# Twelve edge tiles of the first sums, moved from among the last blocks to behind them

## The chip, the cores and the metric

The kernel runs on one core of a Trainium2 chip. The core has a matrix engine (PE, with its weight loads shown apart as PEld), a vector engine (DVE), a scalar engine (ACT), GpSimd (POOL) and a queue processor (SP); transfers run on 16 DMA engines that all queues share. Each engine works through its own list of instructions in order and waits where an input is not there yet. The metric is the device time of one execution in microseconds; lower is better.

## The reference

Two message-passing layers over a graph of 3125 nodes (256 features) and 50000 edges (16 features), sorted by `dst`. The change lies in the first:

```
h   = relu(layernorm(x))
m   = relu(concat(h[src], h[dst], e) @ mW1 + mb1)      # per edge, 512 wide; src is called i, dst j
agg = segment_sum(m @ mW2 + mb2, src)                  # per node
u   = relu(concat(h, agg) @ uW1 + ub1) @ uW2 + ub2
x   = x + h + u
```

It is followed by three graph convolutions over the same edges, with degree scaling, bias and gelu, added to x again. The kernel uses that `segment_sum(m @ mW2)` is `segment_sum(m) @ mW2`, so that only the relu of each edge has to be summed per source node.

## The kernel before

**Two tables, and edges sorted by source.** `h @ mW1` is split by its inputs: `tabA` holds h times the rows for the source, `tabB` h times the rows for the target plus bias. An edge's hidden row before the relu is `tabA[src] + tabB[dst] + e @ wE`. The 50000 edges come as 66 *blocks* of 768 (six groups of 128; the last block holds 80 edges). For each block the kernel forms `tabB[dst] + e @ wE` on PE with one-hot matrices (L642 to L657), copies the result out of PSUM (L660) and scatters it by POOL (L661), six scatters of 128 rows of 528 floats, into `rows_d`, sorted by *node tile*: 25 tiles of 125 source nodes, each with room for 17 groups of 128 edges. A row carries its edge's source and target number behind the 512 values. `window(b)` loads the part of `tabB` that the block needs three blocks ahead on SP's queue (L617); `features(b)` loads edge features on ACT's queue.

**The first sums.** When 26 blocks have been placed, the first 640 rows (`KP` = 5 groups) of every node tile are in place, since later blocks only fill later groups. So from block 26 on a generator, `first_sums`, works on these five groups of each node tile while the other blocks go on. Per node tile t it loads the rows (`xz`, L724, 1320 KB) and 125 rows of `tabA` (L731, 250 KB) on SP's queue, one tile ahead, into two buffers that take turns: the load for tile t+1 has to wait until tile t-1 has been read for the last time. Then come the tile's own steps: target numbers `d_of` (L766), the table rows split in two halves (L245, L246), one-hot matrices of the sources (L769, L770), their transposes on PE (L777, L779), and a copy kept for later in `oh_d` (L781, L782). Then five *edge tiles*, one per group, each one step of the generator: PE spreads the `tabA` rows to the edges (L251), DVE adds the scattered rows (L253, `gb`), ACT and DVE form the relu in two halves `m` (L255, L256), and PE adds them into `p_sum` (L756), one edge tile behind. After the fifth the sum is copied and stored to `R_d` (L759, L760). That makes 25 x 5 = 125 edge tiles.

**Who sets the order.** The generator is advanced by the loop over the blocks: from block `SUMS_AT` = 29 on, after each block, as many steps are taken as the pacing line asks for:

```
if b >= SUMS_AT:
    while n_sums > NT * KP - NT * KP * (b + 1 - SUMS_AT) // (NB - SUMS_AT):
```

Over 37 blocks that is 125 edge tiles, three or four a block, and the last four follow block 65. Program order is not yet the order on the engines: the framework orders each engine's list when the kernel is built, by program order but with steps drawn forward where by its own estimate their inputs are ready. In the trace a tile's `d_of` stands on DVE ahead of the previous tile's third edge tile.

**After the blocks.** A count of failed conditions (L824 to L827) gives `flag`; the branch on it (L1398) starts `messages`, the *message stage*, which has the other twelve groups of each node tile to do (edge tiles again, with L253 to L256 and L1017), counts edges for the second layer and updates the nodes. It loads rows of `rows_d` (L918), which need all scatters in place. Nothing in it can be drawn ahead of the branch. Last come the convolutions, `gcn`.

Of the kernel before, what the change touches and what calls it, by code (L numbers as in the profile page):

```python
# [46 lines left out]
NT, NP = 25, 125  # L47
# [6 lines left out]
NB = (E + BLK - 1) // BLK  # L54
# [6 lines left out]
KP = 5  # L61
FULL_AT = 26
SUMS_AT = 29
MID = 1024
NG, AW = 7, 448
NPAD = NG * AW
# [35 lines left out]
def gnn(ctx: ExitStack, tc: tile.TileContext, x, src, dst, ea, mW1, mb1, mW2, mb2, uW1, ub1, uW2,  # L102
# [160 lines left out]
    with s1:  # L263
# [185 lines left out]
        for a in range(0, NT, TG):  # L449
# [4 lines left out]
            nc.tensor.matmul(p[:, :n], ones_h[:NB, :], Xv[:, v], start=False, stop=True)  # L454
            nc.vector.tensor_scalar(base[:, v], p[:, :n], float(-MID), None, op0=ALU.add)

# [19 lines left out]
        same = l1.tile([P, CN], F32, name="same")  # L476
        nc.gpsimd.tensor_scalar(same, real, float(MID), None, op0=ALU.mult)
        nc.gpsimd.tensor_add(same, same, peers)
# [114 lines left out]
        def features(b0):  # L593
            st[b0] = g1.tile([P, EB, MB * ED], F32, name="ea_st", bufs=2)
            n = min(EB, NB - 1 - b0)
            nc.scalar.dma_start(
                st[b0][:, :n, :].rearrange("p b (h v) -> p (b h) v", h=2),
                ea[b0 * BLK:(b0 + n) * BLK, :].rearrange("(b p j) f -> p b (j f)", p=P, j=MH))
            if b0 + EB >= NB:
                last = st[b0][:, NB - 1 - b0, :]  # L600
                nc.vector.memset(last, 0.0)
                nc.scalar.dma_start(last[P - LEFT:, (MB - 1) * ED:], ea[FULL:, :])
# [4 lines left out]
        def window(b):  # L607
            if b % WG == 0:
                w_now[0] = g1.tile([1, WG, 2], I32, name="w_now", bufs=2)
                c = nc.vector.tensor_copy(w_now[0], w0_i[0:1, b:b + WG, :])  # L610
                if b:
                    tc.add_manual_dep(c.ins, w_now[1].ins.name, SYNC, reason="one group ahead")
            rows, tab = (64 if b < WIDE else P), tabB[b >= EARLY]
            for h in range(2) if b < NB - 1 else (1,):
                reg = nc.sync.value_load(w_now[0][0:1, b % WG, h:h + 1], min_val=0,
                                         max_val=tab.shape[0] - rows)
                o = nc.sync.dma_start(bw[(2 * b + h) % RW][P - rows:, :].bitcast(F32),  # L617
                                          tab[bass.ds(reg, rows), :])
            if b % WG == 0:
                w_now[1] = o  # L620

        def prepare(b):

            rows = pcs[b % 2]
            pc = rows[:, :MB * 64].rearrange("p (k a b f) -> p k a b f", k=MB, a=2, b=2)
            v = st[b // EB * EB][:, b % EB, :].rearrange("p (j f) -> p j f", f=ED)
            v = v.unsqueeze(2).to_broadcast([P, MB, 2, ED])
            nc.vector.tensor_copy(pc[:, :, :, 0, :], v)
            nc.vector.tensor_sub(pc[:, :, :, 1, :], v, pc[:, :, :, 0, :].bitcast(F32))
            rows = rows.bitcast(F32)  # L630
            one[b] = g1.tile([P, MB, P], F32R, name="ohd", bufs=2)
            pay[b] = one[b] if b < WIDE else pays[b % 2]
            a, of = (64, of_high) if b < WIDE else (0, of_row)
            for h in range(2):
                c = slice(h * MH, (h + 1) * MH)
                t = gps.tile([P, H], F32, name="tr")
                for j in range(MH):
                    q = (h * MH + j) * 64
                    nc.tensor.transpose(t[:, j * P:(j + 1) * P], rows[:, q:q + P], ident)
                nc.scalar.copy(pay[b][:64, c, :].rearrange("q j e -> q (j e)"), t[:64, :MH * P])  # L640
                t = gps.tile([P, H], F32, name="bc")
                nc.tensor.matmul(t[:, :MH * P], ident_h[:NB, b:b + 1].to_broadcast([NB, P]),  # L642
                                 near[:, c, :].rearrange("b j p -> b (j p)"), start=True, stop=True)
                made[b] = nc.vector.tensor_scalar(one[b][a:, c, :].rearrange("q j p -> q (j p)"),
                                                  t[a:, :MH * P], of[a:, 0:1], None, op0=ALU.is_equal)

        def block(b):
            z = zt[b % RZ]
            cols = range(MB) if b < NB - 1 else (MB - 1,)
            c = nc.gpsimd.tensor_copy(z[:, :, H:H + 2], ends[:, :, b, :])  # L650
            if b:
                tc.add_manual_dep(c.ins, evicted[b - 1].ins.name, SYNC, reason="scatters before it first")
            for j in cols:
                p = gps.tile([P, H], F32, name="p_z", bufs=3)
                if b >= WIDE:
                    nc.tensor.matmul(p, pay[b][:, j, :], wE, start=True, stop=False)
                nc.tensor.matmul(p, one[b][:, j, :], bw[(2 * b + j // MH) % RW], start=b < WIDE,  # L657
                                 stop=True)
                by = nc.vector.tensor_copy if b < FULL_AT and j in (2, 3) else nc.scalar.copy
                evicted[b] = by(z[:, j, :H], p)  # L660
                s = nc.gpsimd.indirect_dma_start(  # L661
                    out=rows_d, in_=z[:, j, :], in_offset=None,
                    out_offset=bass.IndirectOffsetOnAxis(ap=place[:, j, b:b + 1], axis=0))
                placed(s, b >= FULL_AT)
# [14 lines left out]
        def free_places(t):  # L679
            if t == 0:  # L680
                nc.gpsimd.iota(free_i, pattern=[[1, ND]], base=0, channel_multiplier=ND)
                nc.vector.tensor_copy(free[0], free_i)
                nc.vector.tensor_scalar(free[1], free[0], n_of[:, 0:1], None, op0=ALU.add)
                nc.vector.tensor_scalar(before[:, 0:1], n_of[:, 0:1], -1.0, float(CAP), op0=ALU.mult,
                                        op1=ALU.add)
                return
            nc.vector.tensor_scalar(free[2], free[0], before[:, t - 1:t], n_of[:, t:t + 1],
                                    op0=ALU.is_ge, op1=ALU.mult)
            nc.vector.tensor_add(free[1], free[1], free[2])
            if t < NT - 1:  # L690
                nc.vector.scalar_tensor_tensor(before[:, t:t + 1], before[:, t - 1:t], float(CAP),
                                               n_of[:, t:t + 1], op0=ALU.add, op1=ALU.subtract)
            else:
                nc.vector.tensor_copy(free_i, free[1])

        def no_edges(c):
            with tc.issue_after(scatters[-1].ins):
                s = nc.gpsimd.indirect_dma_start(
                    out=rows_d, in_=zero, in_offset=None,
                    out_offset=bass.IndirectOffsetOnAxis(ap=free_i[:, c:c + 1], axis=0))  # L700
            placed(s, True)
# [95 lines left out]
        for b in range(NB):  # L797
            if b % EB == 0 and b + EB < NB:
                features(b + EB)
            if b + AHEAD < NB:  # L800
                window(b + AHEAD)
            if b + 1 < NB:
                prepare(b + 1)
            if b == FULL_AT:
                ready += scatters
                assert len(ready) == FULL_AT * MB
                sums, n_sums = first_sums(), NT * KP
                next(sums)
            block(b)
            for t in range(5 * b - 5, 5 * b) if 0 < b <= NT // 5 else ():  # L810
                free_places(t)
            if NB - 2 - ND <= b < NB - 2:
                no_edges(b - (NB - 2 - ND))
            for v, n in work:
                while len(v) > max(0, n - n * (b + 1) // FULL_AT):
                    v.pop(0)()
            if b >= SUMS_AT:
                while n_sums > NT * KP - NT * KP * (b + 1 - SUMS_AT) // (NB - SUMS_AT):
                    next(sums)
                    n_sums -= 1  # L820
        assert next(sums, None) is None

        t = small()
# [608 lines left out]
```

## Time and profile before

| what | value |
|---|---|
| median of 4 runs | 2063.13 us (2058.87 to 2065.77) |
| profiled execution | 2065.86 us, its span 2064.1 us |
| first edge tile of the first sums, `gb` | 361.58 us |
| last scatter of the last block | 775.04 us |
| last step of the last edge tile ends | 779.47 us |
| first load of the message stage | 784.89 us |
| first load on the chain of the second layer | 1533.09 us |
| PE, DVE, ACT, POOL busy over the span | 87%, 62%, 52%, 23% |
| blocks 17 to 27, without sums | 7.78 us each |
| blocks 29 to 65, with 125 edge tiles | 414 us together |

How to read the lines of the profile: `L253` is a line of the kernel; `gb<-xz,p_x` is output from inputs; `x2` merges neighbours of the same kind; a bracket gives the idle time before an instruction and what ended it. In a table by stretches each engine's busy time is followed by the number of its instructions, then come the granted clock of PE, the share of the 16 DMA engines that was busy, and GB/s. `SPq` and `ACTq` are transfers being issued by these queues.

### The profile page before, as it was taken

The page shows a single profiled execution, that of the slowest core. Times are in us where ns is not written, and L with a number is a line of the kernel's source. Part 1 is how long each engine was busy: PE and PEld are TensorE (multiplying, and loading weights), DVE is VectorE, ACT ScalarE, POOL GpSimd, SP SyncE. Part 2 cuts the span into 40 slices and gives each one's busy share as a digit, 9 for nine tenths or more (in the row PEclk, how much of TensorE's full clock was granted, in tenths as well). Part 3 has the DMA queues.
Part 4 walks back from the last instruction along what each step waited for, and adds up shares of the span by engine and source line. Part 5 has one row for each costly group of instructions (what it writes and reads, how often), then busy time and mean ns, then how long its engine had stood idle before and what let it go on. Part 6 is the DMA issues. An engine that isn't in the chain of part 4 may idle for free. (4 is left out here: it accounts for less than half of the span.)

```text
span 2064.1 us, 28354 instructions
## 1 busy us (share of the span) xinstructions
PE 1795.2 (87%) x9183; PEld 1410.1 (68%) x9183; DVE 1278.8 (62%) x2931; ACT 1068.0 (52%) x2214; POOL 482.2 (23%) x562
## 2 busy tenths in 40 slices
PE   4788585776767786999999999999979999999997
PEld 1433243454545554788888888888867998999996
DVE  6987243665556566989998889898823233323332
ACT  3445254665656673556555556565536344434432
POOL 6467777655545550000000000000000000000000
PEclk8789797878889897999999999999989999999998
DMA  5679898888888876445454444544221000000111
GB/s 159 232 292 338 316 324 307 300 292 298 296 303 305 314 266 222 159 145 159 149 163 147 144 162 145 162 154 154 87 76 47 1 1 1 1 1 8 34 38 49
DMA packets 182238, 348.27 MB, mean 169 GB/s; under 512 B 38384, under 2 KB 67936, under 8 KB 181690
## 3 DMA queue, kind: packets, MB, share of 16 engines
q1 hardware_dynamic: 112790, 191.30, 29.4%
q0 software_dynamic: 34560, 117.58, 14.9%
q10 hardware_dynamic: 34724, 37.42, 5.3%
q8 instruction: 76, 1.25, 0.2%
q14 instruction: 88, 0.72, 0.1%
HBM read 187.51 MB, written 158.66 MB: 168 GB/s over the span
## 5 line engine op out<-in xcount | busy, mean ns | idle before, releaser
L1278 PE MATMUL p_o<-a,g 125*128 125x448 f32 x2100 | 460.0, 374 | 3.6 <-ACT g L1263 3.4
L661 POOL DMA_INDIRECT rows_d<-zt,place x391 | 393.3, 1006 | 251.7 <-issue 135.5
L1278 PEld LDWEIGHTS p_o<-a,g 125*128 125x128 f32 x2100 | 392.2, 188 | 42.2 <-ACT g L1263 4.6
L255 ACT ACTIVATE m<-gb 128x512 fp32r<-128x512 f32 x425 | 265.5, 632 | 153.8 <-DVE gb L253 111.1
L256 DVE SCALAR_TENSOR_TENSOR m<-gb,m 128x512 fp32r<-128x512 f32 x425 | 287.4, 688 | 31.0 <-ACT m L255 28.5
L1273 ACT CAST a<-A 125x448 fp32r<-125x448 uint8 x263 | 148.6, 566 | 229.3 <-PE p_o L1278 227.8
L1273 DVE CAST a<-A 125x448 fp32r<-125x448 uint8 x262 | 102.8, 393 | 233.3 <-PE p_o L1278 232.3
L1017 PE MATMUL p_sum<-m,oh 128*125 128x512 f32 x600 | 235.8, 436 | 3.1 <-ACT m L255 1.6
L974 PE MATMUL p_A<-od,oh_h 128*126 128x448 f16 (+3 forms) x1000 | 237.4, 327 | 1.2 <-ACT of_src L1005 1.2
L251 PE MATMUL p_x<-apc,ohT 125*128 125x512 f32 x600 | 236.1, 466 | 1.3 <-ACT ohT L950 0.7
L253 DVE TENSOR_TENSOR gb<-z,p_x 128x512 f32<-128x512 f32 x300 | 202.2, 683 | 34.9 <-PE p_x L251 33.6
L660 ACT COPY zt<-p_z 128x512 f32<-128x512 f32 x339 | 182.9, 587 | 63.0 <-PE p_z L657 57.9
L657 PE MATMUL p_z<-bw,ohd 128*128 128x512 f32 x391 | 169.2, 482 | 35.9 <-ACT t_sb L345 16.5
L1226 POOL DMA_DIRECT2D wG<-in_L_gnn_W x3 | 2.2, 745 | 757.4 <-ACT rs_t L218 755.0
L756 PE MATMUL p_sum<-m,hT 128*125 128x512 f32 x250 | 113.6, 501 | 53.9 <-DVE m L256 51.8
L657 PEld LDWEIGHTS p_z<-bw,ohd 128*128 128x128 f32 x391 | 80.2, 215 | 103.5 <-issue 34.8
L974 PEld LDWEIGHTS <-oh_h 128*126 128x126 f16 x1000 | 125.5, 137 | 35.0 <-issue 1.0
L1017 PEld LDWEIGHTS p_sum<-m,oh 128*125 128x125 f32 x600 | 112.3, 189 | 43.9 <-ACT m L255 17.8
L960 DVE TENSOR_SCALAR od<-iota_h,dloc 128x447 f16<-128x447 f16 (+11 forms) x300 | 138.7, 488 | 0.0
L998 ACT CAST A<-p_A 126x448 uint8<-126x448 f32 x175 | 92.9, 531 | 59.5 <-PE p_A L974 58.0
L251 PEld LDWEIGHTS p_x<-apc,ohT 125*128 125x128 f32 x600 | 109.4, 193 | 12.9 <-ACT ohT L950 1.7
L338 PE MATMUL p_z<-wAB,hT 128*128 128x512 f32 (+1 forms) x200 | 108.4, 678 | 8.5 <-ACT hT L321 4.3
(280 smaller groups left out, 2792.0 us busy)
## 6 DMA issues: line engine op xcount, KB each, us to landing
z<-rows_d SPq DMA_DIRECT2D x75, 1056.0 KB
xz<-rows_d SPq DMA_DIRECT2D x25, 1320.0 KB
tabB<-t_sb ACTq DMA_DIRECT2D x26, 512.0 KB
bw<-tabB SPq DMA_DIRECT2D x51, 256.0 KB
bw<-tabB SPq DMA_DIRECT2D x80, 128.0 KB
rows_d<-zt,place POOLq DMA_INDIRECT x391, 6.2
hT<-tabA SPq DMA_DIRECT2D x25, 250.0 KB
R_d<-R_part ACTq DMA_DIRECT2D x25, 250.0 KB
```

What stands on the lines that cost most here:

```text
L251: nc.tensor.matmul(p, ohT, apc[:NP, s, :], start=s == 0, stop=s == 1)
L253: nc.vector.tensor_add(gb, zr, p)
L255: nc.scalar.activation(m[:, 0, :], gb, AF.Relu)
L256: nc.vector.scalar_tensor_tensor(m[:, 1, :], gb, 0.0, m[:, 0, :].bitcast(F32), op0=ALU.max, op1=ALU.subtract)
L657: nc.tensor.matmul(p, one[b][:, j, :], bw[(2 * b + j // MH) % RW], start=b < WIDE, stop=True)
L660: evicted[b] = by(z[:, j, :H], p)
L661: s = nc.gpsimd.indirect_dma_start(out=rows_d, in_=z[:, j, :], in_offset=None, out_offset=bass.IndirectOffsetOnAxis(ap=place[:, j, b:b + 1 ...
L960: nc.vector.tensor_scalar(targets[k][:, :WIDTH[k]], iota_h[:, :WIDTH[k]], d_of[:, t, k:k + 1] if k < KP else dloc[t][:, k:k + 1], None, op ...
L974: nc.tensor.matmul(p_A[g][:, l - g * AW:h - g * AW], oh_h[t][:, k, :], targets[k][:, l - FIRST[k]:h - FIRST[k]], start=start, stop=stop)
L1017: nc.tensor.matmul(p_sum[t], oh, m[:, s, :], start=k == KP and s == 0, stop=k == KT - 1 and s == 1)
L1273: (nc.vector.tensor_copy if turn[0] % 2 else nc.scalar.copy)(a, A[:NP, s, j * AW:(j + 1) * AW])
L1278: nc.tensor.matmul(po[:, f, :AW], g[:, s, q, f * P:(f + 1) * P], a, start=s == 0 and q == 0, stop=s == NT - 1 and q == 1)
```

## The change

A constant `REST_OF` = 12 is added. The pacing line spreads 125 - 12 = 113 edge tiles over blocks 29 to 65, and the twelve that are left are taken one after another behind the last block: the last two of node tile 22 and all ten of tiles 23 and 24. Every instruction of the kernel is still there once.

```
+REST_OF = 12
...
             if b >= SUMS_AT:
-                while n_sums > NT * KP - NT * KP * (b + 1 - SUMS_AT) // (NB - SUMS_AT):
+                while n_sums > NT * KP - (NT * KP - REST_OF) * (b + 1 - SUMS_AT) // (NB - SUMS_AT):
                     next(sums)
                     n_sums -= 1
+        for _ in range(n_sums):
+            next(sums)
         assert next(sums, None) is None
```

## The prediction

> **What bounds the kernel now.** I read the page's forty slices first, to see that the change sits in one stage: slices 7 to 15 (about 360 to 780 us), where the last 37 blocks of edges run beside the first sums. No engine is full there and the DMA engines come nearest, so I asked next for the busy time in stretches of 50 us, then of 3 us.
>
> ```profile
> 600.00:650.00 50.00, 32.59 (x141) 23.16 (x139) 26.38 (x53) 27.07 (x54) 24.81 (x29) 0.87 0.86 306
> 650.00:700.00 50.00, 39.10 (x162) 28.26 (x162) 31.62 (x60) 32.88 (x67) 27.05 (x30) 0.85 0.85 302
> ...
> 711.00:714.00 3.00, 1.78 (x8) 1.07 (x7) 0.00 (x0) 3.00 (x8) 2.09 (x4) 1.00 1.04 416
> 714.00:717.00 3.00, 0.00 (x0) 0.00 (x0) 0.90 (x4) 0.37 (x1) 2.42 (x4) 0.79 1.05 417
> 717.00:720.00 3.00, 2.24 (x6) 1.39 (x6) 3.00 (x7) 0.50 (x1) 2.31 (x2) 0.50 0.62 247
> 720.00:723.00 3.00, 3.00 (x10) 2.32 (x9) 1.28 (x3) 1.82 (x5) 0.73 (x1) 0.57 0.50 192
> ```
>
> The columns are PE, weight load, DVE, ACT, POOL, granted clock, DMA share and GB/s. Over 50 us the DMA engines are 86% busy at some 305 GB/s. Inside that they swing: full while DVE does nothing (711 to 717 us), half idle just after. The waits from 380 to 860 us say what DVE stands for.
>
> ```profile
> DVE d_of L766 <- DMA xz<-rows_d: 99.5, 21, 11.3
> PEld p_sum L756 <- DVE m L256: 80.0, 50, 11.5
> POOL rows_d L661 <- ACT zt L660: 62.3, 53, 11.0
> ```
>
> DVE waits 4.7 us per node tile for the tile's rows (L724), and PE and POOL wait behind it. Last, the time line around the end of the stage, DVE, SP, POOL and ACT alone:
>
> ```profile
> 752.03 0.38 SPq L724 DMA_DIRECT2D xz<-rows_d  x1
> 758.10 1.28 DVE L253 TENSOR_TENSOR gb<-xz,p_x 128x512 f32<-128x512 f32 x2 [0.69 <-PE p_x L251]
> 763.06 0.17 DVE L766 TENSOR_TENSOR d_of<-xz,first 128x5 f32<-128x5 f32 x1 [2.88 <-DMA xz<-rows_d]
> 775.04 0.98 POOL L661 DMA_INDIRECT rows_d<-zt,place  x1 [1.54 <-issue]
> 778.18 1.29 DVE L256 SCALAR_TENSOR_TENSOR m<-gb,m 128x512 fp32r<-128x512 f32 x2
> 780.68 0.27 ACTq L760 DMA_DIRECT2D R_d<-R_part  x1
> 784.89 0.30 SPq L926 DMA_DIRECT2D a_rows<-tabA  x1
> ```
>
> The rows of node tile 24 are asked for at 752.03, when tile 22 has let go of its buffer. Tile 24's first step (763.06) stands on DVE behind only two of tile 23's five edge tiles, so three of them wait for that load too. The last scatter goes out at 775.04, the last edge tile ends at 779.47, its sums are stored at 780.68, and the message stage starts at 784.89, when that store has landed. So the end of the edge tiles sets the start of the next stage, and nothing is left to wait for on POOL.
>
> **The change, part by part.** The pacing line has 113 edge tiles to spread over blocks 29 to 65 and not 125, 3.05 a block and not 3.38. Twelve tiles, 2.4 node tiles of five, come after block 65: the last two of tile 22, and all of 23 and 24. The instructions are the same in number, the flag's steps and the store before the branch keep their place at the end, and the gap from 779.47 to 784.89 stays: 0. So the sum has two terms: what the blocks' stretch loses, and what the tail costs.
>
> *What 2.4 node tiles are worth among the blocks.* From one d_of to the next, from 400.98 to 763.06 us, are 21 periods of 17.24 us with 186 scatters, 8.86 (1.48 blocks) in each. Four neighbours show how they vary; from the first to the fourth they hold 6, 15 and 3 scatters.
>
> ```profile
> 648.21 0.17 DVE L766 TENSOR_TENSOR d_of<-xz,first 128x5 f32<-128x5 f32 x1 [5.98 <-DMA xz<-rows_d]
> 661.20 0.20 DVE L766 TENSOR_TENSOR d_of<-xz,first 128x5 f32<-128x5 f32 x1 [2.17 <-DMA xz<-rows_d]
> 684.39 0.17 DVE L766 TENSOR_TENSOR d_of<-xz,first 128x5 f32<-128x5 f32 x1 [7.55 <-DMA xz<-rows_d]
> 696.77 0.22 DVE L766 TENSOR_TENSOR d_of<-xz,first 128x5 f32<-128x5 f32 x1
> ```
>
> The trace doesn't show a node tile's price by itself, so three ways bound it. (1) By bytes: a node tile moves 1320 KB of rows, 250 of table, 250 of sums and 157.5 of one-hots, 2.025 MB; a block moves six scatters of 270 KB, two windows of 256 KB and 48 KB of features, 2.195 MB. Together 2.025 + 1.48 x 2.195 = 5.27 MB in 17.24 us, 305 GB/s, which is what the stretches show. So a node tile is 6.6 us. (2) By POOL: blocks 17 to 27, without sums, took 7.78 us each, six scatters of 0.96 us with 0.30 between and a copy; 17.24 - 1.48 x 7.78 leaves 5.7 us. (3) A straight line through the periods against their scatters gives 8.5 us + 0.99 us per scatter. I take the bytes, 6.6, because they reproduce the period and DMA is the resource nearest to full. The blocks' stretch ends 2.4 x 6.6 = 15.9 us earlier; ends 13.7 and 20.4. SP's queue is asked for tile 24's rows later, with only the branch behind; ACT's for the stores of tiles 22 to 24, where nothing waits for them but the last.
>
> The Trainium skill, page "DMA: Bandwidth & Descriptors", speaks against the change here: by "Issuing engines are not separate DMA queues" all queues share the same 16 engines, and its Specifications give them a ceiling of 435 GB/s. At that ceiling the 4.86 MB of 2.4 node tiles are worth 11.2 us, and the change would cost 4.7 us more than my sum. The 3 us rows do reach 416 and 417 GB/s, but only in the stretches in which DVE stands; the mean of 305 is what a longer stretch gets.
>
> *What twelve tiles cost alone.* With nothing else on DVE an edge tile takes 1.335 us: the message stage runs pairs of them so.
>
> ```profile
> 800.95 1.28 DVE L253 TENSOR_TENSOR gb<-z,p_x 128x512 f32<-128x512 f32 x2
> 802.41 1.29 DVE L256 SCALAR_TENSOR_TENSOR m<-gb,m 128x512 fp32r<-128x512 f32 x2 [0.19 <-ACT m L255]
> 803.62 1.28 DVE L253 TENSOR_TENSOR gb<-z,p_x 128x512 f32<-128x512 f32 x2
> ```
>
> Two pairs stand 2.67 us apart. Tile 22's last two are 2.7 us. Tile 23: its end is held by tile 24's load, which starts when tile 22 has ended, takes 7.3 us at the least (583.60 to 590.87), then 1.1 us of first steps (0.17, 0.16 and 0.80, partly over each other), then three edge tiles, 4.0: 12.4 us. The shortest period of the trace, 684.39 to 696.77, is 12.4 as well. Tile 24 has no load behind it: five edge tiles, 6.7, and 1.65 of its own steps, 8.3 us. Sum 23.4 us. The low end has the load hidden and 8.3 us for both, 19.3; the high end 12.4 for both, 27.5. None of it has cover: the last scatter lands some 6.2 us (the median of their landings) after its issue, long before the branch, and the stage behind the branch cannot start early. In before the same four tiles stand behind block 65's scatter as in the new order stand ahead of the twelve, so that part cancels.
>
> The same page's "Anatomy of one DMA" fits a transfer of POOL's path with 2.0 us + bytes / 436 GB/s, 5.1 us for these 1320 KB; tile 23 would then take 10.2 us and the sum would be 2.2 us smaller. No load of rows whose landing shows in this stage was that quick, and all had scatters beside them.
>
> **The sum.** 23.4 - 15.9 = +7.5 us, ends 19.3 - 20.4 = -1.1 and 27.5 - 13.7 = +13.8. The profiled execution took 2065.86 us (span 2064.1), so 2073.4 by its own time. It lies 2.7 us over the median of the runs shown, 2063.13; against that median I forecast 2070.7 us.
>
> **Rivals.** *Faster: the loads set the period, and the stalls swallow the blocks.* If a period is load and reaction, then leaving 2.4 periods out saves 2.4 x 17.24 = 41.4 us, and their 3.54 blocks (27.5 us at 7.78) move into the 4.7 us stalls of the other 22.6 periods, where 106 us are to be had. If a share f of them fits there, the change is 23.4 - 41.4 + (1 - f) x 27.5 = 9.5 - 27.5 f: even at f = 0.35, -8.4 us (2054.7) at f = 0.65. For it: the stalls exist, on DVE, in 19 of the last 21 periods. Against it: they are longest (11.3, 9.7, 7.5 us) where the most scatters ran (14, 14, 15), so a stall is no empty place, the DMA engines are full in it.
>
> *Much slower: both ends at once.* The blocks come only down to POOL's 7.78 us and both last tiles pay the full 12.4: +13.8 us, 2076.9. For it: 7.78 held for eleven blocks on end without any sums. Against it: the last tile has no next load to stand for.
>
> *No change.* Either the straight line holds down to no scatters, so that a period costs its 8.5 us wherever it is; or the order on the engines, which is not the program's (d_of stands three edge tiles early), draws the twelve back among the blocks' gaps. Both give 0. Against the first: no period under 12.4 us is seen once the stage runs.
>
> **How the numbers follow.** The forecast (+2 to +13 us, 2065 to 2076) has 0.55, the much slower case 0.15, no change 0.12, faster 0.18. About 0.3%, 6.2 us, is what a measurement of this kernel can tell. Of the forecast's 0.55, 0.38 lies over +6.2 and 0.17 under; of the faster case 0.16 lies under -6.2. So faster 0.16, same 0.17 + 0.12 + 0.02 = 0.31, slower 0.38 + 0.15 = 0.53. The range goes from -8 to +16 us, 2055 to 2079: it leaves out the deeper half of the faster case and the worst of the much slower one.
>
> **What the new profile would show.** Right: the last scatter some 16 us earlier, near 759; then about 28 us in which POOL and the DMA engines are nearly idle and DVE runs edge tiles, with one stall of 3 to 5 us at a d_of; the first a_rows load of the message stage near 792; everything after it unchanged and later by the same amount; periods among the blocks near 18.2 us with 9.7 scatters. Wrong: the last scatter over 23 us earlier with d_of stalls well under 4.7 us (the faster rival), or under 14 us earlier with periods over 18.5 (the slower one); edge tiles of 23 and 24 ahead of block 65's matmuls (no change). The forecast also fails if the new pacing makes the engines' order fall differently against the loads all along the stage: periods here differ by 10 us and more, and a sum of means doesn't see that.

## The result and the profile after

The changed kernel takes 2071.0 us (median of 42 runs, 2062.8 to 2080.1); the kernel before took 2062.8 us in 68 runs beside it. The ratio is 1.0043, 95% interval 1.0033 to 1.0053, so the change costs some 8 to 9 us. The forecast was 2070.7 us.

The profiled execution of the changed kernel took 2072.48 us (span 2070.7). Lines of its code are one higher up to L820 of the kernel before, three higher behind it. These times, read from the time lines, cut both spans into the same pieces:

| us | before | after | difference |
|---|---|---|---|
| start to the first gb of the first sums | 361.6 | 355.7 | -5.9 |
| first gb to the last scatter | 413.5 | 389.0 | -24.5 |
| last scatter to the first load of a_rows | 9.9 | 40.1 | +30.2 |
| first load of a_rows to the end of the span | 1279.2 | 1286.0 | +6.8 |

Two rows belong to the change: the blocks end earlier and the tail is longer, together +5.7 us. The first and the last row hold the same instructions in the same order on every engine in both kernels. In the nine other traces of kernels that do the whole work (those below, and these two again) the last piece took 1279.3 to 1284.6 us, so those two rows show how far executions differ, and they nearly cancel.

Stretches of 50 us in the blocks, and the tail as one stretch (columns: PE, weight load, DVE, ACT, POOL, clock, DMA share, GB/s):

```profile
600.00:650.00 50.00, 36.75 (x149) 25.48 (x147) 26.33 (x50) 30.01 (x60) 27.08 (x30) 0.84 0.87 299
650.00:700.00 50.00, 40.71 (x173) 29.64 (x174) 32.11 (x62) 33.89 (x68) 28.89 (x33) 0.85 0.86 295
744.00:780.00 36.00, 27.14 (x83) 15.43 (x82) 26.16 (x46) 17.75 (x32) 1.32 (x2) 0.87 0.42 145
```

Among the blocks the DMA share is what it was, 0.86 to 0.87 (0.85 to 0.86 before). In the tail POOL is all but empty, and no engine is full: PE is busy for 27.14 of 36 us, DVE for 26.16. The waits from 380 to 860 us:

```profile
DVE d_of L767 <- DMA xz<-rows_d: 79.8, 20, 7.8
PEld p_sum L757 <- DVE m L257: 56.1, 57, 7.2
POOL rows_d L662 <- ACT zt L661: 42.4, 46, 6.0
```

The wait for the rows of a node tile fell from 99.5 to 79.8 us in all, to 4.0 a time from 4.7. And the time line of the tail, chosen rows of all engines:

```profile
742.14 0.17 DVE L767 TENSOR_TENSOR d_of<-xz,first 128x5 f32<-128x5 f32 x1 [3.82 <-DMA xz<-rows_d]
744.62 0.98 POOL L662 DMA_INDIRECT rows_d<-zt,place  x1 [0.28 <-POOL zt L651]
745.52 0.36 SPq L725 DMA_DIRECT2D xz<-rows_d  x1
746.12 0.29 SPq L732 DMA_DIRECT2D hT<-tabA  x1
754.14 0.16 DVE L767 TENSOR_TENSOR d_of<-xz,first 128x5 f32<-128x5 f32 x1
755.71 0.36 SPq L725 DMA_DIRECT2D xz<-rows_d  x1
757.33 0.62 ACT L246 CAST hT<-hT 125x512 fp32r<-125x512 f32 x1 [2.96 <-DMA hT<-tabA]
757.85 0.62 ACT L256 ACTIVATE m<-gb 128x512 fp32r<-128x512 f32 x1
758.53 0.79 PE L757 MATMUL p_sum<-m,hT 128*125 128x512 f32 x1 [2.88 <-ACT m L256]
762.21 0.69 DVE L254 TENSOR_TENSOR gb<-xz,p_x 128x512 f32<-128x512 f32 x1 [2.94 <-PE p_x L252]
766.09 0.16 DVE L767 TENSOR_TENSOR d_of<-xz,first 128x5 f32<-128x5 f32 x1
778.33 0.69 DVE L257 SCALAR_TENSOR_TENSOR m<-gb,m 128x512 fp32r<-128x512 f32 x1 [0.72 <-ACT m L256]
780.23 0.26 ACTq L761 DMA_DIRECT2D R_d<-R_part  x1
784.70 0.30 SPq L929 DMA_DIRECT2D a_rows<-tabA  x1
```

The last scatter goes out at 744.62, not 775.04, and 16 edge tiles start behind it, 14 more than the two before (the first of the 16 starts 0.2 us behind it): the engines' order draws block 65 two tiles further ahead. Three d_of's stand 12.0 us apart, the last m ends at 779.02, and the next stage starts at 784.70, 5.7 us behind it (5.4 before). No d_of waits for rows in the tail. What stands there is each tile's start. ACT waits 2.96 us at L246 for a row of tabA (of the 25 such casts this is the last, so it is tile 24's), whose load was asked for at 746.12 behind 1320 KB of rows. Tile 22's last relu (757.85) is behind that cast in ACT's list, PE's next sum (758.53) and the transposes of tile 23 behind it wait for that relu, and DVE stands 2.94 us for the first p_x of tile 23.

### The profile page after: what moved, and what is told of

Same layout as the page of the kernel before. It is cut to its first block, busy times and chain, and to the rows that moved or that the text cites. A ratio compares the mean times of both kernels' runs of the same rounds, so it can differ in the third digit from the quotient of the medians.

```text
span 2070.7 us, 28365 instructions
## 1 busy us (share of the span) xinstructions
PE 1807.9 (87%) x9183; PEld 1413.4 (68%) x9183; DVE 1282.0 (62%) x2931; ACT 1069.5 (52%) x2214; POOL 480.7 (23%) x562
## 5 line engine op out<-in xcount | busy, mean ns | idle before, releaser
L1020 PEld LDWEIGHTS p_sum<-m,oh 128*125 128x125 f32 x600 | 112.2, 189 | 48.2 <-ACT m L256 20.4
L252 PE MATMUL p_x<-hT 125*128 125x512 f32 x250 | 96.2, 461 | 35.1 <-DVE gb L254 34.4
L252 PEld LDWEIGHTS p_x<-apc,ohT 125*128 125x128 f32 x600 | 109.5, 193 | 12.5 <-DVE gb L254 1.5
```

The costliest lines, as they stand in the source:

```text
L252: nc.tensor.matmul(p, ohT, apc[:NP, s, :], start=s == 0, stop=s == 1)
L1020: nc.tensor.matmul(p_sum[t], oh, m[:, s, :], start=k == KP and s == 0, stop=k == KT - 1 and s == 1)
```

## The experiments

Three theories were left. The first: the cost is linear, a node tile being worth less among the blocks than it takes alone. The second: the cost is a fixed one at the seam, such as the wait for table rows just seen. The third: the loads of rows set the blocks' periods, and the blocks would run faster if those came earlier.

**Twice as many tiles behind the blocks** (rest24).

```diff
-REST_OF = 12
+REST_OF = 24
```

> Twenty-four edge tiles behind the blocks and not twelve. If the cost is (tail price - price among the blocks) per edge tile, it doubles: 8.2 us for twelve, so 15 to 18 us over before, about 2079. Rival, a fixed cost of starting a tail or of the new order: the same 8 us, about 2071. Rival, the second dozen comes cheaper since the blocks then run near POOL's 7.78 us: below +12 us.

Measured: 2077.33 us against 2062.36, ratio 1.0068 (1.0046 to 1.0090), +15.0 us by the medians, 14.0 by the ratio. Twelve more tiles cost another 5 to 7 us, which speaks for a cost in the tiles. The interval just overlaps that of the change, so the times alone hardly exclude a fixed cost; that is left to the traces of all pacings, below. Once the tail has settled, its d_of's stand 9.3, 9.5 and 9.7 us apart (DVE):

```profile
747.09 0.16 DVE L767 TENSOR_TENSOR d_of<-xz,first 128x5 f32<-128x5 f32 x1
756.36 0.17 DVE L767 TENSOR_TENSOR d_of<-xz,first 128x5 f32<-128x5 f32 x1 [1.07 <-DMA xz<-rows_d]
762.48 1.42 DVE L254 TENSOR_TENSOR gb<-xz,p_x 128x512 f32<-128x512 f32 x2 [1.57 <-PE p_x L252]
765.90 0.16 DVE L767 TENSOR_TENSOR d_of<-xz,first 128x5 f32<-128x5 f32 x1
771.96 0.69 DVE L254 TENSOR_TENSOR gb<-xz,p_x 128x512 f32<-128x512 f32 x1 [1.39 <-PE p_x L252]
775.64 0.16 DVE L767 TENSOR_TENSOR d_of<-xz,first 128x5 f32<-128x5 f32 x1
```

A node tile alone is thus five edge tiles of 1.335 us, its own first steps, and 1.3 to 1.8 us in which DVE stands for the first p_x. The stall for rows is 1.07 us at most.

**The table row asked for first** (tables_first), to shorten the seam's wait.

```diff
 def rows_of(t):
+    a = a_rows[t % 2]
+    nc.sync.dma_start(a, tabA[t * NP:(t + 1) * NP, :])
...
-    a = a_rows[t % 2]
-    nc.sync.dma_start(a, tabA[t * NP:(t + 1) * NP, :])
```

> The changed kernel with one swap: each node tile's 250 KB of the table is asked for before its 1320 KB of rows, on the same queue. In the trace of the changed kernel ACT stands 2.2 and 3.0 us in the tail for the table rows, with relus of the tile before behind it. If that wait holds the tail: 3 to 6 us under the changed kernel, about 2066. Rival, the tail's 12 us per node tile is the load of the rows and the chain behind it, and the wait on ACT only fills time: no change, 2071 within 2 us.

Measured: 2073.26 us, ratio 1.0060 (1.0037 to 1.0084). ACT's two waits in the tail shrank from 2.2 and 3.0 to 1.1 and 1.5 us, and the d_of's there came 11.9 and 9.3 us apart, so the tail gained. The blocks lost as much: from the first gb to the last scatter 391.8 us, not 389.0. The 3 to 6 us that this wait should have been worth did not show in the time, so the theory that it is what the change costs falls, as far as halving the wait can tell.

**Tiles drawn forward** (early8): the pacing of before, with the first sums done eight tiles earlier.

```diff
-while n_sums > NT * KP - NT * KP * (b + 1 - SUMS_AT) // (NB - SUMS_AT):
+while n_sums > max(0, NT * KP - (NT * KP + 8) * (b + 1 - SUMS_AT) // (NB - SUMS_AT)):
```

> The other direction: the pacing line hands out 133 edge tiles where there are 125, so that the sums are through some two blocks before the last and no edge tile follows block 65. If the cost per edge tile behind the blocks goes on with the other sign (0.7 us each), the four that stand behind block 65 in before are worth 2 to 3 us: 2060, and the message stage then starts when the last scatter has landed. Rival, more edge tiles per block lengthen the loads' stalls: 2 to 6 us over before. Rival, the order decides and not the count: either sign, more than 5 us.

Measured: 2063.44 us, ratio 1.0000 (0.9980 to 1.0019). No edge tile is left behind the last scatter, and a_rows is asked for 3.1 us after it, not 9.9; the blocks take 419.2 us, not 413.5. What the end gains, the blocks lose: what is drawn out of the tail is paid for among the blocks. It isn't better than before, and no kernel here that does the whole work is.

These traces give the price that the trace of before alone did not. D is the mean time from one d_of to the next, from the fourth to the one nearest to the last scatter, N the scatters in it:

| kernel | D, us | N | D - 0.99 N | wait for rows per d_of |
|---|---|---|---|---|
| early8 | 16.81 | 8.33 | 8.56 | 3.8 |
| before | 17.24 | 8.86 | 8.47 | 4.3 |
| after | 18.28 | 9.89 | 8.48 | 4.0 |
| tables_first | 18.56 | 10.05 | 8.61 | 4.1 |
| rest24 | 19.47 | 11.06 | 8.52 | 4.0 |

With the slope found in the periods of before, 0.99 us per scatter, a node tile is worth 8.5 us at every pacing; a line through the five rows alone gives the same 0.99 and 8.5. The stretches say it without a slope per scatter. From the first gb to the last scatter early8, before, after, tables_first and rest24 took 419.2, 413.5, 389.0, 391.8 and 369.7 us, with 125, 123, 109, 108 and 97 edge tiles started by then: a line through them has 1.72 us per edge tile, 8.6 per node tile, 20.6 for twelve edge tiles, and misses single traces by up to 2.7 us. What follows, up to the first load of a_rows, grows from 9.9 us in before (2 edge tiles) to 65.2 in rest24 (28), 2.13 us each, 25.6 for twelve. The difference, 0.41 us per edge tile, makes 5 us for twelve. The wait per d_of stays near 4 us while N grows by a third: the stalls did not take up the blocks.

**The twelve tiles left out** (omit12b, omit12c, omit12d are the same kernel on three chips), to measure both prices without a model.

```diff
-for t in range(NT):
+KS = {t: KP if t < 22 else 3 for t in range(23)}
+for t in KS:
...
-        for _ in range(n_sums):
-            next(sums)
...
-    nc.sync.dma_start(R[t], R_d[t * NP:(t + 1) * NP, :])
+    u = min(t, 22)
+    nc.sync.dma_start(R[t], R_d[u * NP:(u + 1) * NP, :])
```

> The changed kernel without its tail: 113 edge tiles beside the blocks (node tile 22 ends after three of its five), and the twelve that follow block 65 are left out altogether; the message stage reads sums, one-hots and target numbers of node tile 22 in place of those of 23 and 24, so it has the same work to do. It measures the first term by itself, what 2.4 node tiles are worth among the blocks. Prediction's term: 15.9 us less than before, ends 13.7 and 20.4, so about 2047 us. Theory after the two traces (last scatter 30 us earlier, 25 us if counted from the first node tile's start): both terms were taken too small, and it is 22 to 28 us under before, about 2038. Rival, the loads set the period: up to 41 us under before. Rival, the cost comes from the engines' new order and not from the tail: less than 10 us under before.

> The changed kernel without its tail again (113 edge tiles beside the blocks; the message stage reads node tile 22's sums, one-hots and target numbers for tiles 23 and 24), on one chip with the changed kernel and the one before. The time of the changed kernel over this one is the price of the tail, the time of the one before over this one the price of 2.4 node tiles among the blocks. On a chip with 7.78 us blocks: 20 to 28 us under before (prediction's term: 15.9). On one where blocks without sums take 10 us: within 5 us of before, as in the second set, since the scatters then hold the stretch.

> The changed kernel without its tail (113 edge tiles beside the blocks; the message stage reads node tile 22's sums, one-hots and target numbers for tiles 23 and 24) a third time, for a chip on which blocks without sums take 7.78 us, if it meets one. There the prediction's term says 15.9 us under before (13.7 to 20.4); the two traces' last scatters, 25 to 30 us earlier, would say 22 to 28. If it meets a chip with 10 us blocks: within 5 us of before, as twice already.

Measured: 2125.68 us, ratio 1.0004 (0.9983 to 1.0025); 2120.77 us, ratio 0.9984 (0.9965 to 1.0002); 2128.20 us, ratio 1.0004 (0.9983 to 1.0026). Leaving the tiles out gained nothing in the time. On these three chips the kernel before itself took some 2124 us, and there the price of the result does not apply; the last section shows what differs. The two kernels were therefore run again on one of them.

**Before and after again, beside the kernel without the tiles** (before_again, after_again, the copies unchanged).

> The kernel before once more, for a second trace of it and for the interval of a kernel against itself: 0 within 0.2%. On the chip of the second set of runs the front of the kernel (up to the first edge tile) took 419 to 426 us and not 356 to 362, and blocks without sums some 10 us and not 7.78; on the first chips 356 to 362 again.

> The changed kernel once more, on the same chip as the other three. Theory, the cost is the tail's time less what the blocks' stretch gains: +8 us (+6 to +11) on a chip like the first; on one like that of the second set, where leaving the twelve out gained nothing, +10 to +24 us.

Measured on the chip of omit12c, with before at 2123.26 us: before_again 2121.65, ratio 0.9983 (0.9963 to 1.0003); after_again 2141.12, ratio 1.0090 (1.0062 to 1.0117). The change costs 18 to 19 us there, twice as much. After_again and omit12c have the same blocks with the same 113 tiles; among the first sums they differ by the twelve tiles of the tail (the rows of tile 23 are still loaded in omit12c), and that is 2141.12 - 2120.77 = 20.4 us (22.5 by the ratios). But the end of omit12c has a wait of its own. Its last copy of a sum, and that of before_again:

```profile
832.01 0.58 ACT L761 COPY R_part<-p_sum 125x512 f32<-125x512 f32 x1 [5.11 <-DMA R_d<-R_part]
```

```profile
836.30 0.58 ACT L759 COPY R_part<-p_sum 125x512 f32<-125x512 f32 x1 [1.31 <-PE p_sum L756]
```

Tile 22 ends there after three edge tiles, so close behind tile 21 that the copy into R_part, which has one buffer, waits until tile 21's store has landed. From the end of the last m to the copy 4.4 us pass, not 0.6 as in before_again: some 3.8 us (4.2 and 3.2 in omit12b and omit12d) are omit12c's own. With them the tail's price is 24 to 26 us, and before_again over omit12c, 0.9 us, becomes some 5 us that the twelve tiles are worth among the blocks of that chip: little, but not nothing.

**Ten tiles done twice** (again10): tiles 23 and 24 once more behind block 65, with the pacing of before.

```diff
-for t in range(NT):
+SEQ = [*range(NT), NT - 2, NT - 1]
+for i, t in enumerate(SEQ):
...
+        for _ in range(2 * KP):
+            next(sums)
```

> The kernel before with node tiles 23 and 24 done a second time behind the last block (ten edge tiles more, with their loads and stores, the same values written again): the tail's price alone, with the blocks' stretch as before. By the prediction's terms 12.4 + 8.3 = 20.7 us; by the trace of the changed kernel, 12.0 us from one d_of to the next, 24 us. If it is near 8 us, work behind the blocks costs less than thought, and the change's cost lies among the blocks.

Measured: 2146.98 us, ratio 1.0107 (1.0080 to 1.0134), +23.7 us, 11.9 for each node tile behind the blocks. The tail of the change is 2.4 such tiles at 10 to 11 each.

**A third buffer for the rows** (xz3), with loads two tiles ahead, and the change on top of it (xz3_rest12). To make room, RZ goes from 4 to 3; rz3 is that alone.

```diff
-RZ = 4
+RZ = 3
...
-v = g1.tile([P, XZ], F32, name="xz", bufs=2)[:, :KP * ZW]
+v = (g1.tile([P, XZ], F32, name="xz", bufs=2)[:, :KP * ZW] if t % 3 < 2
+     else p1.tile([P, KP * ZW], F32, name="xz_3"))
...
-if 0 < t < NT - 1:
-    loaded[t + 1] = rows_of(t + 1)
+if 0 < t < NT - 2:
+    loaded[t + 2] = rows_of(t + 2)
```

> Control for the next kernel: the kernel before with three buffers for a block's rows ahead of the scatter and not four. If the scatters' backlog matters little: within 4 us of before. If POOL then runs dry while DVE stands: 5 to 15 us slower.

> The kernel before with a third buffer for a node tile's rows, loaded two tiles ahead (its room comes from the fourth block buffer, as in the control). If the loads' time sets the period and bytes have room, DVE's 4.7 us per node tile mostly go and the stage is 30 to 60 us shorter, about 2015 to 2030. If bytes set the pace, as the prediction's price of a node tile has it (305 GB/s reproduces the period), the stalls go but the blocks take as long: within 10 us of the control.

> The change on top of the third buffer. With the load of the last tiles long landed, the tail's node tiles should fall from 12 us towards DVE's 8.3 us, and the cost of the change from 8 us to about 3 us or less over the kernel with three buffers. If the price of a node tile among the blocks falls as well (no stalls left), the cost stays at 5 to 10 us.

Measured, with before at 2124.0 us on that chip: rz3 2128.04, ratio 1.0013 (0.9993 to 1.0034); xz3 2130.95, ratio 1.0034 (1.0012 to 1.0055); xz3_rest12 2141.90, ratio 1.0066 (1.0043 to 1.0089). The waits of xz3 and of its control rz3, from 380 to 860 us:

```profile
DVE d_of L767 <- DMA xz<-rows_d: 37.5, 15, 8.5
```

```profile
DVE d_of L766 <- DMA xz<-rows_d: 43.5, 15, 4.9
```

A load asked for a whole period earlier took only a little of the wait away, and the kernel got no faster. So the buffer does not hold the blocks on these chips. The change costs 11 us on top of xz3 by the medians, 7 by the ratios, and not the 3 us or less that were expected if the loads were its cost. On the chips of the result xz3 was not run, so there this rests on the table above.

## Why the prediction was right, by its own steps

**The sum is right within some 2 us; by the traces its two terms are not.** Both were taken too small, and the errors cancel: that the sum came so near is luck.

*What 2.4 node tiles are worth among the blocks* was put at 15.9 us, by bytes, 6.6 us a tile. By the five traces this is the term that was mis-sized most: a node tile costs 8.5 us there, which is the forecast's way 3, and 2.4 tiles 20.4 us, its upper end. Way 1 was chosen because it reproduces the period of 17.24 us. It does that because the rate of 305 GB/s was taken from the same stretch: it shares one time out over two kinds of work, and can't say which of the two holds it. Five pacings can. The last scatter came 30.4 us earlier on the time line, not 16: 5.9 us of that is the front, 20.4 the twelve tiles, 3.4 (two fifths of 8.5) the two tiles more behind block 65, and 0.7 are not accounted for.

*The Trainium skill's ceiling* in "DMA: Bandwidth & Descriptors", 435 GB/s in its Specifications, would have priced the tiles at an estimated 11.2 us. The blocks ran at 295 to 299 GB/s after the change, and the term went the other way, to 20.4. Rates near the ceiling, 416 and 417 GB/s, are in two rows of 3 us of the forecast; no row of 50 us shows them.

*What twelve tiles cost alone* was put at 23.4 us. In the trace, counted from the end of one gb to the end of another, they took 25.3 us, inside the stated ends: tile 22's last two 3.5 (752.22 to 755.69; forecast 2.7), tile 23 12.5 (to 768.24; forecast 12.4), tile 24 9.3 (to 777.56; forecast 8.3). Tile 23's number is right, but not for the forecast's reason, as the next paragraph says. The sum of DVE's steps left out the 1 to 3 us at each tile's start in which DVE waits for p_x, 2.94 us at tile 23 and 1.06 at tile 24. That chain runs over ACT and PE, has no DVE time and so no row in a sum of DVE's durations. The direct measurement, on the other chip, gave 24 to 26.

*The four tiles ahead of the twelve* were said to cancel, since four follow block 65 in both programs. On the engines they don't: in before two edge tiles start behind the last scatter and end 3.0 us after it was issued (775.04 to 778.00), in the changed kernel four stand there ahead of the twelve, and they take 7.6 us (744.62 to 752.22). These 4.6 us and the 25.3 make up the 30 us by which the tail is longer; in return the blocks have two edge tiles less, 3.4 us.

*The load in the tail.* The stall of 3 to 5 us at a d_of was not there; what stands is ACT at L246 and, behind it, DVE before p_x. In rest24, 18 us behind the last scatter, a row load was asked for at 748.66 and let d_of go at 756.36, 7.7 us. That is with no scatter beside it, and near the forecast's 7.3 us. The 5.1 us estimated from the Trainium skill's "DMA: Bandwidth & Descriptors", section "Anatomy of one DMA", a fit for POOL's path and not for SP's, did not appear.

*The periods* were put at 18.2 us with 9.7 scatters and came at 18.28 with 9.89. That reading tells little: it follows from 66 blocks and 113 tiles whichever of the ways is true, as long as the blocks' stretch is near its forecast.

*The rivals.* Faster asked for stalls to swallow the blocks; they stayed at 4 us per d_of, and xz3 gained nothing. "No change", in its form that a period costs its 8.5 us wherever it is, is half true: 8.5 us among the blocks at every pacing is what was found, but alone the tile costs 9.3 to 9.7 once settled and 12 at the seam. "Much slower" came true on the chips on which before takes 2124 us, and nearly by its own mechanism: POOL's scatters hold the blocks there, though at 1.9 us each and not at the 1.3 of a 7.78 us block, and a node tile done twice behind the blocks took 11.9 us.

**What stays open.** The cost is the tail's price less the price among the blocks. By the traces of the two kernels that is 30.2 - 24.5 = +5.7 us for fourteen edge tiles, by the five traces 5 us for twelve, by the times 8 to 9 (6.8 to 10.9 by the interval). The tail measured directly, 24 to 26, less the cost of 8 to 9 us leaves 15 to 18 for the 2.4 tiles among the blocks: near the forecast's 15.9, and under the 20.4 of the traces. The tail's price is from another chip than the rest, and the kernel without the twelve tiles never ran on a chip like that of the result. So that a node tile is worth 8.5 us there, and that 15.9 was too small, is read from five traces of one execution each, and not measured by leaving it out.

## What to carry to other kernels

Moving work out of an overlapped stage costs the difference of two prices, its price beside the other work and its price alone, and each is only known from a run with another amount of it: vary the pacing, and fit the period against the work in it. A resource that is 86% busy over a stage does not price the work in it by its bytes, since that shares one measured time out by assumption. To price a step alone, follow its chain through every engine from its first load to its last result; the durations of one engine leave out what it waits for at each start. And a kernel from which work is left out can have a wait of its own where the work stood: read its trace there before its time is taken for a price.

## What was not expected of the hardware

The same kernel takes 2062 us on some chips and 2122 to 2127 on others, and the 60 us lie in the blocks ahead of the first sums. The later kernels all met the slower kind, each set on another chip; no chip is known to have been met twice, so that it is the chip and not the hour is not shown. From the start to the first gb it takes 356 to 362 us on the one kind and 418 to 430 on the other. POOL's waits from 250 to 340 us, first the kernel before, then before_again:

```profile
POOL rows_d L661 <- issue: 9.8, 32, 0.3
```

```profile
POOL rows_d L661 <- issue: 34.2, 36, 9.2
```

"Issue" is time in which the engine waited for nothing that the profile shows. On the second chip POOL stands so four times in these 90 us, for 2.6 to 9.2 us at a time; one of them, between two scatters:

```profile
320.71 0.21 POOL L650 COPY zt<-ends 128x12 f32<-128x12 f32 x1
327.17 0.98 POOL L661 DMA_INDIRECT rows_d<-zt,place  x1 [6.25 <-issue]
```

And the DMA engines are less busy, not more (100 to 400 us, before, then before_again):

```profile
100.00:400.00 300.00, 218.34 (x697) 113.82 (x697) 160.06 (x384) 140.72 (x281) 217.84 (x244) 0.84 0.87 314
```

```profile
100.00:400.00 300.00, 210.58 (x565) 99.62 (x565) 133.97 (x349) 108.87 (x214) 181.57 (x204) 0.78 0.71 258
```

A block without sums takes 7.78 us on the first and 9.8 to 10.4 on the mean on chips of the second kind. There the scatters seem to set the stage: among the blocks with sums the time per scatter is 1.86 to 1.91 us at every pacing (before_again 16.78 us for 8.81 scatters, after_again 18.37 for 9.89, omit12c 18.55 for 9.79). Sums among the blocks cost little then: the nine traces of that kind have 16.7 to 17.0 us for 8.8 to 8.9 scatters and 18.4 to 18.8 for 9.8 to 10.0, and a line through them leaves an estimated 2.8 us per node tile, 7 for 2.4, beside the 5 from the times. Twelve tiles taken to the end then cost most of their tail. This fits that the change costs 18 to 19 us there and 8 to 9 on the others. What holds POOL was not found. The traces of that kind tell no landing of a scatter (in the trace of the kernel before its median is 6.2 us after the issue), so a wait for an earlier scatter's landing would be called "issue" there as well; that was not tested. What a stage hides on one chip it need not hide on another.
